# Conv and attention in fp32: 140 unused products of zeros between the attention and the last output projections

## The chip, the core and the metric

The kernel runs on one core of one Trainium2 chip, in one launch. The metric is the device time of a whole execution in microseconds (us). Before the change two runs took 2857.51 and 2857.95 us, median 2857.73 us.

## What is computed

The input `x` has 4 images of 384 channels and 48 x 48 positions, so 4 x 2304 tokens. All of it is fp32.

```python
local = depthwise_conv_7x7(x) * bn_scale + bn_shift
qkv   = layernorm(x_tokens) @ qkv_w.T + qkv_b          # 8 heads of 48
q     = q + layernorm(local_tokens)
out   = softmax(q @ k.T * 48**-0.5) @ v
y     = x + (out @ proj_w.T + proj_b)
```

## The kernel before

**Tiling.** A group `t` is 384 tokens (`G`), six groups to an image, 24 in all (`NT`). For each group the kernel goes over 4 pairs of heads `p` and 18 key blocks `kb` of 128 keys. `score` (L786) makes four products of 64 keys x 384 queries for a pair and a block (L795), and ScalarE takes the exponential of the two banks at once (L803). `weigh` (L808) makes the four products of the values with these exponentials (L816). Each of these products uses a quarter of TensorE's array: 48 or 64 rows by 64 columns. `project` (L501, its matmul is L503) makes the linear layers with the whole 128 x 128 array, three products to one 128 x 384 result, and the last three outputs of a group go through `finish` (L768), where VectorE adds bias and residual (L771) and ScalarE's queue sends the store (L774). `columns` (L618, its matmul is L624), at the start, has products of one row by 128 columns, with the row in three different strips of 32 partitions.

In the trace every fp32 product leaves two MATMUL records and two LDWEIGHTS records, so the x counts there are twice the number of products.

**PSUM.** There are two rings of two buffers, each buffer two banks: `ring()` (named r) and `accumulator()` (named o). `two_banks()` (L96) takes from them in turn.

**Order.** PE, DVE and ACT run in the order in which the code is written (`manual_schedule`, L84 and L85); the queues of SP and POOL are ordered by the scheduler. VectorE's depthwise convolution is dealt out by a plan over points between the attention's steps; none of it is left when the last group `t` = 23 is attended.

**Where the change goes.** After the last attention step stand

```python
    rest()
    pair_out()
    pair_add()
    for before in range(NT - NG, NT):
```

`rest` (L835) issues the last `weigh`, `pair_out` (L690) copies the last pair's first bank (L702, ACT), `pair_add` (L704) adds the second one (L711, DVE) and sends the denominators off (L714 and L718, SP). The loop then makes the output projections of the last image's six groups: 9 products each, with `two_banks()` twice. `divide` (L722) of the last group and its scaling (L1094) are issued inside this loop behind the first and the third group's `finish`; the sixth projection needs them. The tiles with the tags `k0` and `k1` of the pool `big` hold keys of the token groups 0 and 1 of the image in work.

Of the kernel before, what the change touches and what calls it, by code (L numbers as in the profile page):

```python
# [10 lines left out]
F32 = mybir.dt.float32  # L11
# [4 lines left out]
P = 128  # L16
# [29 lines left out]
def unshifted_pass(  # L46
# [16 lines left out]
    nc = tc.nc  # L63
# [3 lines left out]
    CC = C // P  # L67
    G = RG * W
# [10 lines left out]
    big = ctx.enter_context(tc.tile_pool(name="big", bufs=1))  # L79
# [16 lines left out]
    def two_banks():  # L96
        return next(either)()
# [80 lines left out]
    for c in range(CC):  # L178
        for r, n, first in ((0, HD, 0), (64, HD, 1), (48, 16, 6), (112, 16, 7)):
            head = first + 2 * c if first < 6 else first  # L180
            ch = head * HD + (16 * c if first >= 6 else 0)
            while n:
                part = min(n, P - ch % P)
                pieces.append((c, r, ch // P, ch % P, part))
                r, n, ch = r + part, n - part, ch + part
# [315 lines left out]
    def project(dst, weights, src, n=G):  # L501
        for c in range(CC):
            nc.tensor.matmul(dst, lhsT=weights(c), rhs=src(c), start=c == 0, stop=c == CC - 1)  # L503
# [85 lines left out]
    rows = {}  # L589
# [28 lines left out]
    def columns():  # L618

        r, r2 = two_banks(), two_banks()  # L620
        m = {1: r[:, 0, 0:CC], 2: r[:, 1, 0:CC], 0: r2[:, 0, 0:CC]}
        for i in m:
            for c in range(CC):
                nc.tensor.matmul(  # L624
                    m[i][:, c : c + 1],
                    lhsT=row[of_row(i), c * P : (c + 1) * P],
                    rhs=one[of_row(i)],
                    start=True,
                    stop=True,
                )  # L630
        return m, r2[:, 1, :G]
# [58 lines left out]
    def pair_out():  # L690

        if not ended:
            return
        t, p, sums = ended[0]
        if p == 0:
            ao = work.tile([P, CC, G], F32, tag="ao", name=f"ao{t}")
            ao3 = work.tile([P, G], F32, tag="aot", name=f"aot{t}", bufs=1)
            den = dram.tile([NH, G], F32, tag="den", name=f"den{t}")
            outputs[t] = ao, ao3, den
        ao, ao3, den = outputs[t]  # L700
        dst = ao[:, p, :] if p < CC else ao3
        nc.scalar.copy(dst[0 : 64 + HA], sums[0 : 64 + HA, 0, :G])  # L702

    def pair_add():  # L704

        if not ended:
            return
        t, p, sums = ended.pop()
        ao, ao3, den = outputs[t]
        dst = (ao[:, p, :] if p < CC else ao3)[0 : 64 + HA]  # L710
        nc.vector.tensor_add(dst, sums[0 : 64 + HA, 1, :G], dst)  # L711
        for j in range(2):
            r = 64 * j
            nc.sync.dma_start(out=den[2 * p + j : 2 * p + j + 1], in_=dst[r + HD : r + HA])  # L714
        if p == NP - 1:
            for c in range(CC):
                for r in (0, 64):
                    nc.sync.dma_start(  # L718
                        out=ao[r + HD : r + 64, c, :], in_=ao3[r + 16 * c : r + 16 * c + 16]
                    )  # L720

    def divide(t):  # L722

        few = NH * G // P
        rd = work.tile([P, few], F32, tag="rd", name="rd")
        rb = work.tile([P, CC, G], F32, tag="rb", name="rb", bufs=1)
        rden = dram.tile([NH, G], F32, tag="rden", name=f"rden{t}")
        nc.sync.dma_start(out=rd, in_=outputs[t][2].rearrange("h (k f) -> (h k) f", f=few))
        nc.vector.reciprocal(rd, rd)

        for bound, op in ((SAFE, ALU.is_le), (1 / SAFE, ALU.is_ge)):
            nc.vector.scalar_tensor_tensor(inside, rd, bound, inside, op, ALU.mult)
        nc.sync.dma_start(out=rden.rearrange("h (k f) -> (h k) f", f=few), in_=rd)
        heads = rden[0:6].rearrange("(c h) n -> h c n", h=2)
        for j in range(2):
            r = 64 * j
            last = rden[6 + j : 7 + j].rearrange("o (x n) -> o x n", x=1)
            nc.sync.dma_start(
                out=rb[r : r + HD], in_=heads[j : j + 1].to_broadcast([HD, CC, G])
            )  # L740
            nc.sync.dma_start(out=rb[r + HD : r + 64], in_=last.to_broadcast([16, CC, G]))
        return rb
# [25 lines left out]
    def finish(t, co, m, queue=nc.sync):  # L768
        b, g = divmod(t, NG)
        xr = residuals[t]  # L770
        nc.vector.scalar_tensor_tensor(  # L771
            xr[:, co, :], m, pb[:, co : co + 1], xr[:, co, :], ALU.add, ALU.add
        )
        queue.dma_start(  # L774
            out=out[b, co * P : (co + 1) * P, g * G : (g + 1) * G], in_=xr[:, co, :]
        )
# [4 lines left out]
    halves = [slice(64 * i, 64 * i + 64) for i in range(2)]  # L781
# [26 lines left out]
    def weigh():  # L808
        nonlocal sums
        t, p, kb, pt = weighing.popleft()  # L810
        if kb == 0:
            sums = accumulator()
        for i, h in enumerate(halves):
            for j in range(2):
                first = (kb % NB * NH + 2 * p + j) * HA
                nc.tensor.matmul(  # L816
                    sums[halves[j], i, :G],
                    lhsT=values[t // NG, kb // NB][h, first : first + 64],
                    rhs=pt[h, j, :],
                    start=kb == 0,  # L820
                    stop=kb == KB - 1,
                )
        if kb == KB - 1:
            ended.append((t, p, sums))

    def attend(t, s, half):
# [3 lines left out]
        for kb in range(k0 + n * half, k0 + n * half + n):  # L830
            score(t, p, kb)
            if len(weighing) > LAG:
                weigh()

    def rest():  # L835
        while weighing:
            weigh()
        while jobs:
            jobs.popleft()()
# [52 lines left out]
    m, bank = columns()  # L892
# [57 lines left out]
    for t in range(NT):  # L950
        b, g = divmod(t, NG)
        if g == 0 and b:
# [4 lines that stand above are left out]
# [46 lines left out]
        for s in range(NSLOT):  # L1003
# [66 lines left out]
            if following and s == first + 1:  # L1070
                norm.sum_squares()
                if t:
                    norm.out()

    rest()
    pair_out()
    pair_add()
    for before in range(NT - NG, NT):
        ao = aos[before % NG]
        if before == NT - NG + 3:  # L1080
            judge[1](two_banks()[:, 0, :])
        r, r2 = two_banks(), two_banks()
        parts = r[:, 0, :G], r[:, 1, :G], r2[:, 0, :G]
        for co, m in enumerate(parts):
            project(m, lambda c: w_o[:, c, co * P : (co + 1) * P], lambda c: ao[:, c, :])
        for co, m in enumerate(parts):
            finish(before, co, m, nc.scalar)
        if before == NT - NG:
            rb = divide(NT - 1)
            judge[0]()  # L1090
        if before == NT - NG + 3:
            judge[2]()
        if before == NT - NG + 2:
            nc.vector.tensor_mul(outputs[NT - 1][0], outputs[NT - 1][0], rb)  # L1094
        if before == NT - 2:
            n_outside = judge[3]()
# [3 lines left out]
def conv_attention(tc: tile.TileContext, *args):  # L1100
    nc = tc.nc
    few = NH * RG * 48 // P
    with tc.tile_pool(name="keep", bufs=1) as keep:
        inside = keep.tile([P, few], F32, tag="inside", name="inside")
        outside = keep.tile([P, few], F32, tag="outside", name="outside")
        ones = keep.tile([P, 1], F32, tag="ones_col", name="ones_col")
        total = keep.tile([1, 1], F32, tag="total", name="total")
        flag = keep.tile([1, 1], mybir.dt.int32, tag="flag", name="flag")
        counts = []
        nc.vector.memset(inside, 1.0)  # L1110
        nc.vector.memset(ones, 1.0)

        def compare():
            nc.vector.tensor_scalar(outside, inside, 0.5, None, ALU.is_lt)

        def count(m):
            counts.append(m[0:1, :few])
            nc.tensor.matmul(counts[0], lhsT=ones, rhs=outside, start=True, stop=True)

        def decide():  # L1120
            nc.vector.tensor_reduce(total, counts[0], AX.X, ALU.add)
            nc.vector.tensor_copy(flag, total)

        def read():
            return nc.values_load(flag[0:1, 0:1])

        n_outside = unshifted_pass(tc, *args, inside, (compare, count, decide, read))
        with tc.If(n_outside > 0):
            shifted_pass(tc, *args)
# [505 lines left out]
```

## Time and profile before

| what | value |
|---|---|
| median of 2 runs | 2857.73 us |
| span of the profiled execution, first to last instruction | 2857.6 us |
| mean granted TensorE clock | 0.997 |
| PE busy | 2838.7 us, 99% of the span |
| PE weight loads (PEld) busy | 1778.1 us, 62% |
| VectorE busy | 2344.6 us, 82% |
| ScalarE busy | 1649.5 us, 58% |
| last attention product on PE starts | 2816.62 us |
| first record of the last projections | 2817.03 us |
| last VectorE instruction starts | 2852.51 us |

The profiled execution shows no time of its own outside its span, so 2857.6 us is compared with the median of 2857.73 us.

How to read it: a row of a timeline has start, length, engine, source line, operation, result<-operands, rows*columns of the array for TensorE, shapes and the number of instructions merged into it. "L816" is line 816 of the kernel. The length of a MATMUL record is modelled and has a latency in it, so what one product takes in a stream is read from the distance between starts, or from the chain of waits, whose rows have start, length, engine, line and count. PEld is the load of weights, which can run under the matmul before it.

### The profile page before, as it was taken

To read this page: it belongs to the slowest core of one execution; us is meant where nothing else is said; L and a number is where in the kernel's file an instruction comes from. 1 tells how busy PE (TensorE), PEld (TensorE's weight loads), DVE (VectorE), ACT (ScalarE), POOL (GpSimd) and SP (SyncE) were. 2 spreads that over 40 slices of the span, in tenths; PEclk is the share of its full clock that TensorE was granted. 3 is DMA by queue.
4 is the path that set the end of the run, shared out by engine and by line. 5 is a ranking of instruction groups with operands and counts; after the bars stand their busy time and mean duration, and the time that the engine had idled before them with its cause. 6 is when DMAs were issued, how large, how long until landed. Compare 5 with 4: busy or idle time off the path is not lost.

```text
span 2857.6 us, 70328 instructions
## 1 busy us (share of the span) xinstructions
PE 2838.7 (99%) x29558; PEld 1778.1 (62%) x29558; DVE 2344.6 (82%) x4635; ACT 1649.5 (58%) x2350; POOL 14.9 (1%) x77
## 2 busy tenths in 40 slices
PE   9999999999999999999999999999999999999999
PEld 5544444654554466666655546888875545788886
DVE  7899999999888988878888889887788787887401
ACT  4366666666226666666622666666652366666662
POOL 1000000000000000000000000000000000000000
PEclk9999999999999999999999999999999999999999
DMA  5101121112231211121132112101113211111111
GB/s 106 40 5 36 45 49 35 36 26 43 71 83 25 46 35 41 31 39 24 38 94 70 28 30 50 36 22 37 44 25 94 53 20 29 43 23 32 46 38 63
DMA packets 103433, 123.71 MB, mean 43 GB/s; under 512 B 43136, under 2 KB 89152, under 8 KB 103104
## 3 DMA queue, kind: packets, MB, share of 16 engines
q1 hardware_dynamic: 99568, 115.48, 17.0%
q8 instruction: 234, 3.83, 0.6%
q10 hardware_dynamic: 2992, 3.62, 0.4%
q14 instruction: 95, 0.78, 0.1%
q0 software_dynamic: 544, 0.01, 0.0%
HBM read 81.39 MB, written 27.03 MB: 38 GB/s over the span
## 4 chain that ended last, share of the span: by engine, by line
PE 92%; DVE 6%; DMA 0%; POOL 0%; ACT 0%; issue 0%; DVEq 0%; ACTq 0%; POOLq 0%
PE o L816 37%; PE r L795 37%; PE o L503 9%; PE r L503 9%; DVE acc L284 5%; DMA pb<-in_proj_b_dram 0%; PE r L299 0%; PE r L412 0%; ACT pt L803 0%; DVE sq L401 0%; DVE xn L681 0%; DMA parts<-part 0%; DVE sq L400 0%; POOL qk_vec L167 0%; DVE acc L672 0%
## 5 line engine op out<-in xcount | busy, mean ns | idle before, releaser
L803 ACT ACTIVATE pt<-r 128x768 f32<-128x768 f32 x1728 | 1399.6, 810 | 760.1 <-PE r L795 743.6
L284 DVE SCALAR_TENSOR_TENSOR acc<-slab,vec,acc 128x368 f32<-128x368 f32 (+6 forms) x3447 | 1756.3, 582 | 1.2
L816 PE MATMUL o<-pt,v 64*64 64x384 f32 x13824 | 1544.7, 483 | 0.0
L795 PE MATMUL r<-xn,k 48*64 48x384 f32 x10368 | 1157.8, 483 | 3.7 <-ACT pt L803 3.7
L816 PEld LDWEIGHTS o<-pt,v 64*64 64x64 f32 x13824 | 715.3, 133 | 406.7 <-issue 224.0
L795 PEld LDWEIGHTS r<-xn,k 48*64 48x64 f32 x10368 | 531.9, 133 | 316.2 <-issue 176.1
L795 PE MATMUL r<-qt,kt 48*64 48x384 f32 x3456 | 388.1, 482 | 0.1
L795 PEld LDWEIGHTS r<-qt,kt 48*64 48x64 f32 x3456 | 181.3, 133 | 99.1 <-issue 43.8
L711 DVE TENSOR_TENSOR ao<-o,ao 113x384 f32<-113x384 f32 x72 | 39.9, 554 | 194.0 <-PE r L795 176.8
L503 PE MATMUL o<-xn,w_qk 128*128 128x384 f32 x450 | 153.3, 486 | 0.0
L503 PE MATMUL r<-xn,w_qk 128*128 128x384 f32 x414 | 141.1, 486 | 0.0
L503 PEld LDWEIGHTS o<-xn,w_qk 128*128 128x128 f32 x450 | 85.5, 190 | 59.6
L503 PEld LDWEIGHTS r<-xn,w_qk 128*128 128x128 f32 x414 | 78.7, 190 | 54.8
L536 ACT COPY v<-r 128x384 f32<-128x384 f32 x42 | 18.2, 482 | 126.9 <-PE r L503 126.9
L503 PE MATMUL r<-w_v,xn 128*128 128x384 f32 x252 | 85.2, 487 | 0.0
L711 DVE TENSOR_TENSOR aot<-o,aot 113x384 f32<-113x384 f32 x24 | 13.3, 556 | 82.4 <-ACT aot L702 64.8
L503 PE MATMUL o<-af,w_o 128*128 128x384 f32 x222 | 75.0, 487 | 0.0
L400 DVE TENSOR_TENSOR sq<-sq 128x384 f32<-128x384 f32 x47 | 26.0, 554 | 57.7 <-ACT sq L395 56.2
L503 PEld LDWEIGHTS r<-w_v,xn 128*128 128x128 f32 x252 | 47.6, 190 | 34.4 <-issue 1.8
L503 PE MATMUL o<-w_v,xn 128*128 128x384 f32 x180 | 64.4, 498 | 1.3 <-ACT w_v L635 1.3
L503 PEld LDWEIGHTS o<-af,w_o 128*128 128x128 f32 x222 | 42.1, 190 | 29.2
L771 DVE SCALAR_TENSOR_TENSOR xr<-r,pb,xr 128x384 f32<-128x384 f32 x27 | 16.4, 617 | 51.8 <-ACT xn L555 41.9
(139 smaller groups left out, 1036.9 us busy)
## 6 DMA issues: line engine op xcount, KB each, us to landing
xr<-in_x_dram SPq DMA_DIRECT2D x24, 576.0 KB
slab<-in_x_dram SPq DMA_DIRECT2D x32, 378.0 KB
held<-ao SPq DMA_DIRECT2D x20, 576.0 KB
af<-held SPq DMA_DIRECT2D x20, 576.0 KB
rb<-rden SPq DMA_DIRECT2D x48, 216.0 KB
out_dram<-xr SPq DMA_DIRECT2D x54, 192.0 KB
xn<-in_x_dram SPq DMA_DIRECT2D x46, 216.0 KB
slab<-in_x_dram SPq DMA_DIRECT2D x14, 297.0 KB
```

The costliest lines, as they stand in the source:

```text
L284: nc.vector.scalar_tensor_tensor(dst, src, weight, dst, ALU.mult, ALU.add)
L400: nc.vector.tensor_add(self.buf[:, 0, :], src[:, 0, :], src[:, 1, :])
L503: nc.tensor.matmul(dst, lhsT=weights(c), rhs=src(c), start=c == 0, stop=c == CC - 1)
L536: nc.scalar.copy(v[:, blk, :, 0:HD], r[:, :C].rearrange("p (h d) -> p h d", d=HD))
L711: nc.vector.tensor_add(dst, sums[0 : 64 + HA, 1, :G], dst)
L771: nc.vector.scalar_tensor_tensor(xr[:, co, :], m, pb[:, co : co + 1], xr[:, co, :], ALU.add, ALU.add)
L795: nc.tensor.matmul(r[h, j, :G], lhsT=kk[:, blk * P + h.start : blk * P + h.stop], rhs=qq, start=True, stop=True,)
L803: nc.scalar.activation(pt, r[:, :, :G], AF.Exp, scale=SCALE)
L816: nc.tensor.matmul(sums[halves[j], i, :G], lhsT=values[t // NG, kb // NB][h, first : first + 64], rhs=pt[h, j, :], start=kb == 0, stop=kb ...
```

## The change

A new function `halves_first` is called between `pair_add()` and the last loop. It fills two tiles with zeros on POOL, one declared float32r and one fp32, under the tags `k0` and `k1`, and issues products of them into PSUM buffers that nobody reads. In order: 24 float32r products of 64 x 128 row tiles that alternate between the upper and the lower rows (`j`) with new weights for each pair; 24 with two moving tiles per weights, `j` innermost; 24 with `j` outside, so that the same rows come twice in a row; 12 float32r products of the whole array; and four rounds of 6 row-tile products followed by 8 fp32 products of 64 x 64. That is 108 float32r products and 32 fp32 ones. The results of the reference are computed as before.

```diff
+    def halves_first():
+
+        part = big.tile([P, CC, G], mybir.dt.float32r, tag="k0", name="part_r")
+        whole = big.tile([P, CC, G], F32, tag="k1", name="whole_f")
+        nc.gpsimd.memset(part.bitcast(F32), 0.0)
+        nc.gpsimd.memset(whole, 0.0)
+
+        def rows(j):
+            return slice(64 * j, 64 * j + 64)
+
+        def row_tile(r, j, w, m):
+            nc.tensor.matmul(
+                r[:, j, :G],
+                lhsT=part[rows(j), w, 0:P],
+                rhs=part[rows(j), m, :],
+                start=True,
+                stop=True,
+            )
+
+        def quad(r):
+            for j in range(2):
+                for h in halves:
+                    nc.tensor.matmul(
+                        r[h, j, :G],
+                        lhsT=whole[rows(j), 0, h],
+                        rhs=whole[rows(j), 1, :],
+                        start=True,
+                        stop=True,
+                    )
+
+        r = two_banks()
+        for i in range(12):
+            for j in range(2):
+                row_tile(r, j, i % 3, (i + 1) % 3)
+        r = two_banks()
+        for i in range(6):
+            for m in range(2):
+                for j in range(2):
+                    row_tile(r, j, i % 3, m)
+        r = two_banks()
+        for i in range(6):
+            for j in range(2):
+                for m in range(2):
+                    row_tile(r, j, i % 3, m)
+        r = two_banks()
+        for i in range(12):
+            nc.tensor.matmul(
+                r[:, i % 2, :G],
+                lhsT=part[:, i % 3, 0:P],
+                rhs=part[:, (i + 1) % 3, :],
+                start=True,
+                stop=True,
+            )
+        for n in range(4):
+            r = two_banks()
+            for w, m in ((0, 0), (0, 1), (1, 2)):
+                for j in range(2):
+                    row_tile(r, j, w, m)
+            r = two_banks()
+            for _ in range(2):
+                quad(r)
...
     rest()
     pair_out()
     pair_add()
+    halves_first()
     for before in range(NT - NG, NT):
```

## The prediction, made before the changed kernel ran

> **What bounds the kernel now.** I read the busy times first, then the chain of waits around the place of the change, then single rows there. Busy times of the page and its chain by engine:
>
> ```profile
> PE 2838.7 (99%) x29558; PEld 1778.1 (62%) x29558; DVE 2344.6 (82%) x4635; ACT 1649.5 (58%) x2350; POOL 14.9 (1%) x77
> PE 92%; DVE 6%; DMA 0%; POOL 0%; ACT 0%; issue 0%; DVEq 0%; ACTq 0%; POOLq 0%
> ```
>
> TensorE is full and carries the chain. An average says nothing of the last 40 us, where the change goes, so here is the chain there (start, length, what):
>
> ```profile
> 2813.87 0.65 PE o L816 x4
> 2814.52 0.65 PE r L795 x4
> 2815.17 1.94 PE o L816 x18
> 2817.11 4.07 PE r L503 x12
> 2821.17 1.94 PE o L503 x6
> 2823.11 3.87 PE r L503 x12
> ...
> 2850.53 1.95 PE r L503 x6
> 2852.48 0.02 issue
> 2852.51 0.62 DVE xr L771
> ```
>
> PE is the chain up to 2852.48 with no gap in it. So whatever PE does at 2817.1 is added to the end in full. Three prices stand in these rows. Six whole-array fp32 products (12 records) take 3.87 us in a stream: 0.645 each, 0.3225 a record. Four 64 x 64 fp32 products take 0.65 us together (0.648), as long as one whole-array product: the four quarters of the array work side by side. And the first projection row has 4.07 where a later one has 3.87: 0.20 us is the price of going from quarters to the whole array. Its parts are in the timeline (start, length):
>
> ```profile
> 857.40 0.49 PE L503 MATMUL o<-ao,w_o 128*128 128x384 f32 x1
> 857.82 0.53 PE L795 MATMUL r<-xn,k 48*64 48x384 f32 x1
> 2816.62 0.48 PE L816 MATMUL o<-pt,v 64*64 64x384 f32 x2
> 2817.03 0.19 PEld L503 LDWEIGHTS r<-af,w_o 128*128 128x128 f32 x1 [0.60 <-issue]
> 2817.03 0.59 PE L503 MATMUL r<-af,w_o 128*128 128x384 f32 x1
> ```
>
> Last record to first load is 0.41 to 0.42 in both directions, of which 0.32 is streaming: 0.09 of drain. Then the first load is bare, and the first record is that much longer than its kind: 0.59 against 0.49, so about 0.105 with 128 columns, and 0.53 against 0.48, so 0.05 with 64. A switch costs 0.20 into 128 columns and 0.14 into 64.
>
> **What the Trainium skill says.** "TensorEngine Tiling (Array Packing)", Tiling Modes: changing the mode drains the engine, and tiles load and multiply independently. The rows above agree: 0.09 us of drain, four quarters in the time of one. "FP8 and Floating Point Precision", TensorE Precision Notes: fp32 takes four passes; a reduced form reads 4 bytes and truncates. The first agrees, 0.645 / 4 = 0.161 us for a pass of 384; no float32r product is in this trace. "TensorE: Matmul & The Clock Gate", Back-to-back issue gap: 384 / 2.4 + 2.5 ns = 0.1625 us, an estimate from that page beside 0.161 measured. Same page, LDWEIGHTS: columns / 1.2, so 0.107 us for 128, beside the 0.105 above.
>
> **The change part by part.** Nothing is removed. In the built program the products stand in the written order between L816 and the first L503; DVE and ACT keep their order, SP keeps its own, and POOL gets two memsets behind all its others.
>
> *POOL.* A 128 x 128 memset took 0.205 us, so nine times that is about 1.9 us each. They wait for the last readers of the keys in `k0` and `k1`: pair 2, blocks 2 and 5 of the last group. Block 17 of that pair is scored at about 2791, a block each 1.30 us, so these are at about 2772 and 2776. Both memsets are done by about 2778, nearly 40 us ahead of their reader. Cost nothing; late, they would show as a wait of PE for POOL.
>
> *Buffers.* The first `r` and `o` are free as they are today. The fourth call (the whole-array part) takes the accumulator of the last pair and waits for L711, done at 2818.2; it starts after 6 us of row tiles. Later calls wait for PE's own writes four calls back, done long before. Twelve calls keep the turn of r and o as it was. Cost nothing.
>
> *A pass in float32r.* I take one pass, 0.161 us; the bounds are one and four (0.645). *Row tiles.* Two of 64 x 128 take the rows and columns that four quarters take in the attention, and write two banks side by side as those do, so I take 0.161 a pair. That asks for a 128-column load per tile and pass. Two places speak to it: packing, 14 records of 50 moving columns on the whole array (a row of the groups), and `columns`, 18 records of one moving column in three strips (four rows of the timeline).
>
> ```profile
> L207 PE MATMUL o<-natural,packing 128*128 128x50 f32 x14 | 1.7, 270 | 0.0
> ```
>
> ```profile
> 32.20 0.74 PE L624 MATMUL o<-one,row 1*128 1x1 f32 x8
> 32.70 0.27 PE L624 MATMUL r<-one,row 1*128 1x1 f32 x1
> 32.78 0.27 PE L624 MATMUL o<-one,row 1*128 1x1 f32 x2
> 33.06 0.47 PE L624 MATMUL r<-one,row 1*128 1x1 f32 x3
> ```
>
> Packing is bound by its loads: (1.7 - 0.27) / 13 = 0.11 us a load, under the 0.161 of a pass, so it hides in one array. In `columns` all 18 start between 32.20 and about 33.28, 1.1 us where one after another would need 2.0: 128-column loads of different row strips overlap, and the third strip (r) starts before the second (o) is through its list. So a strip whose list is held up doesn't stop the next, which is what the third order needs. As to issue, a pair of row tiles asks for two load-and-multiply records in 0.161 us; the attention has eight in 0.648, the same rate.
>
> *The sum.* Three orders: 3 x 12 pairs x 0.161 = 5.81. Whole array: 12 x 0.161 = 1.94. Four rounds: 4 x 3 pairs x 0.161 = 1.94 and 8 sets of four fp32 quarters x 0.645 = 5.16. Switches: six into 128 columns (first order, whole array, four rounds) x 0.197 = 1.18, four into 64 columns x 0.144 = 0.58; the last one into the projections is paid today. Together 16.6 us.
>
> *Behind it.* All six projections, their `finish` and their stores move by the same 16.6 us, and with them `divide`, which stands behind the first group's L771 on DVE. Its reply is needed at 2846, after a scaling that ends at 2836.6: almost 10 us of slack that keep their size. The last store (5 us from L771 to the end of the span) moves along. So 2857.6 + 16.6 = 2874.2 for the profiled execution; the median of the runs shown is 0.1 above the span: 2874.3.
>
> **The rivals.**
> *Row tiles take turns*, for a bank, a queue or float32r's own reasons, in some or all orders. For it: no trace shows a float32r tile, and the third order sends two of a tile in a row. Against it: `columns` and the quarters. All: 48 passes more, +7.7, 2882.1 us; one order alone: +1.9, 2876.3.
> *Loads come bare*, if float32r's load can't go under a pass: 60 slots (48 pairs, 12 whole) x 0.11 = +6.6, 2880.9. Against it: the loads of L503 start with the matmul before.
> *Four passes*: 60 x 3 x 0.161 = +29.0, 2903.3. Against it: the change is named single-pass, as the page has it of the reduced form.
> *Cheaper switches*: 64 x 64 and 64 x 128 split the rows alike; if going between them doesn't drain, eight switches fall (4 x 0.197 + 4 x 0.144 = 1.4): 2872.9. Nothing here shows this pair.
> *The other side, slower by over 2%*: every row-tile product drains before the next starts, because it changes tile. Price: drain 0.09, bare load 0.105, pass 0.161, and the latency of a record beyond its streaming, 0.486 - 0.3225 = 0.164: 0.52 us. 96 x 0.52 = 49.9, with 1.94, 5.16 and 0.8 of switches 57.8: 2915.5. It decides from 0.51 us a product. Against it: quarters change tile at every product and don't.
> *It does nothing or something else* (products not run, something in the tail gained): 2857.7. They stand in the built program; PE has no slack to hide them.
>
> **How the numbers follow.** About what a measurement can tell from no change is 2%, 57 us. Chances: the forecast 0.62 (its own range, from 15 to 19 us added: 2872.7 to 2876.7), cheaper switches 0.08, turns 0.14, bare loads 0.08, four passes 0.04, a drain each 0.02, nothing or else 0.02. The range from 2872.3 to 2882.6 holds the first four, 0.92, and ends there because turns in all orders sit at its upper end. Over 2% slower: the drain, and four passes together with turns (2934), 0.02. Faster by 2%: 0.01. Within: 0.97.
>
> **What would show it.** In the profile after: L846 (row tiles) with starts of both tiles within 0.02 us and 1.94 us for each of the three orders, the same for all three; L881 1.94 us; L857 0.645 for four; 0.09 us between the last streaming and the next load at each change of mode; no wait of PE for POOL; the first L503 at about 2833.6 instead of 2817.03 and the rows behind it as far apart as now. An order at 3.9 us means turns, at 3.2 bare loads, at 7.7 four passes. The prediction is wrong if PE's rows there are not the chain, or if the projections behind come out longer.

## The result, and the profile after

Two runs of the changed kernel took 2878.47 and 2880.12 us, median 2879.3, against 2857.73 before: ratio 1.0074, 95% interval 1.0045 to 1.0104. In five later runs (e2 below), beside 17 of the kernel before, it took 2875.9 against 2858.88: 1.0060, interval 1.0047 to 1.0074. The forecast was 2874.3 us, with a range from 2872.3 to 2882.6 that left room for rivals, and from 2872.7 to 2876.7 for the forecast alone.

The profiled execution has a span of 2876.6 us; that same run took 2878.47. Between 1.7 and 1.9 us lie outside the span in every run for which both are known, so a span is compared with a span from here on, and a run with a run. For the kernel before, the profiled execution and the two timed runs were different executions: a span of 2857.6 us beside a median of 2857.73 doesn't mean that nothing lies outside the span.

The page after, busy times and the chain by engine:

```profile
PE 2858.0 (99%) x29730; PEld 1834.7 (64%) x29730; DVE 2344.1 (81%) x4635; ACT 1650.0 (57%) x2350; POOL 17.0 (1%) x79
PE 93%; DVE 6%; ACT 0%; DMA 0%; issue 0%; SPq 0%; DVEq 0%; ACTq 0%
```

PE has 172 records more: 108 for the float32r products, one each, and 64 for the 32 fp32 ones, two each. So a float32r product isn't split into two records as an fp32 one is. The chain of waits at the place of the change (start, length, what):

```profile
2816.61 1.94 PE o L816 x17
2818.54 2.28 PE r L846 x24
2820.83 2.08 PE o L846 x24
2822.91 2.08 PE r L846 x24
2824.99 2.29 PE o L881 x12
2827.28 0.72 PE r L846 x6
2828.00 1.45 PE o L857 x16
...
2833.80 0.72 PE r L846 x6
2834.52 1.45 PE o L857 x16
2835.97 4.07 PE r L503 x12
2840.03 1.94 PE o L503 x6
2841.97 3.87 PE r L503 x12
```

What the reader is to see: the inserted rows fill 2818.54 to 2835.97, 17.43 us, with no gap; the three orders take the same 2.08 (the first one has the switch of 0.20 on top); and from L503 on every row has the length it had before, the 4.07 of the first one too. The last L771 starts at 2871.37 and the span ends 5.2 us later, as before (5.1). POOL's two memsets are the rows

```profile
2774.03 1.06 POOL L839 MEMSET part_r<- 128x1152 f32 x1 [654.70 <-PE r L795]
2777.92 1.06 POOL L840 MEMSET whole_f<- 128x1152 f32 x1 [2.83 <-PE r L795]
```

done at 2779, nearly 40 us ahead of their reader.

### The profile page after: what moved, and what is told of

Its sections match the earlier page's. It is cut to its first block, busy times and chain, and to the rows that moved or that the text cites. A ratio compares the mean times of both kernels' runs of the same rounds, so it can differ in the third digit from the quotient of the medians.

```text
span 2876.6 us, 70682 instructions
## 1 busy us (share of the span) xinstructions
PE 2858.0 (99%) x29730; PEld 1834.7 (64%) x29730; DVE 2344.1 (81%) x4635; ACT 1650.0 (57%) x2350; POOL 17.0 (1%) x79
## 4 chain that ended last, share of the span: by engine, by line
PE 93%; DVE 6%; ACT 0%; DMA 0%; issue 0%; SPq 0%; DVEq 0%; ACTq 0%
PE r L795 37%; PE o L816 37%; PE o L503 9%; PE r L503 9%; DVE acc L284 5%; PE r L846 0%; PE r L299 0%; PE o L857 0%; DMA staged<-in_qkv_wT_dram 0%; ACT pt L803 0%; PE r L412 0%; SPq L104 0%; DVE sq L401 0%; DMA slab<-in_x_dram 0%; DVE sq L400 0%
## 5 line engine op out<-in xcount | busy, mean ns | idle before, releaser
L816 PE MATMUL o<-pt,v 64*64 64x384 f32 x13824 | 1565.5, 483 | 0.0
L795 PE MATMUL r<-xn,k 48*64 48x384 f32 x10368 | 1171.6, 483 | 3.9 <-ACT pt L803 3.9
L816 PEld LDWEIGHTS o<-pt,v 64*64 64x64 f32 x13824 | 740.4, 133 | 384.7 <-issue 198.6
L795 PEld LDWEIGHTS r<-xn,k 48*64 48x64 f32 x10368 | 549.4, 133 | 299.2 <-issue 159.2
L795 PE MATMUL r<-qt,kt 48*64 48x384 f32 x3456 | 394.5, 482 | 0.1
L795 PEld LDWEIGHTS r<-qt,kt 48*64 48x64 f32 x3456 | 188.0, 133 | 93.9 <-issue 33.2
L503 PE MATMUL o<-xn,w_qk 128*128 128x384 f32 x450 | 154.3, 488 | 0.0
L503 PE MATMUL r<-xn,w_qk 128*128 128x384 f32 x414 | 141.0, 486 | 0.0
L503 PEld LDWEIGHTS o<-xn,w_qk 128*128 128x128 f32 x450 | 86.1, 191 | 60.5 <-issue 1.5
L503 PEld LDWEIGHTS r<-xn,w_qk 128*128 128x128 f32 x414 | 78.7, 190 | 54.9
L503 PE MATMUL r<-w_v,xn 128*128 128x384 f32 x252 | 85.2, 487 | 0.0
L711 DVE TENSOR_TENSOR aot<-o,aot 113x384 f32<-113x384 f32 x24 | 13.4, 556 | 82.4 <-ACT aot L702 64.8
L771 DVE SCALAR_TENSOR_TENSOR xr<-r,pb,xr 128x384 f32<-128x384 f32 x27 | 16.4, 617 | 73.2 <-ACT xn L555 44.8
L503 PE MATMUL o<-af,w_o 128*128 128x384 f32 x222 | 75.0, 486 | 0.0
L503 PEld LDWEIGHTS r<-w_v,xn 128*128 128x128 f32 x252 | 47.6, 190 | 34.4 <-issue 1.8
L503 PE MATMUL o<-w_v,xn 128*128 128x384 f32 x180 | 66.6, 512 | 1.8 <-ACT w_v L635 1.8
L503 PEld LDWEIGHTS o<-af,w_o 128*128 128x128 f32 x222 | 42.1, 190 | 29.2
```

The costliest lines, as they stand in the source:

```text
L771: nc.vector.scalar_tensor_tensor(xr[:, co, :], m, pb[:, co : co + 1], xr[:, co, :], ALU.add, ALU.add)
L795: nc.tensor.matmul(r[h, j, :G], lhsT=kk[:, blk * P + h.start : blk * P + h.stop], rhs=qq, start=True, stop=True,)
L816: nc.tensor.matmul(sums[halves[j], i, :G], lhsT=values[t // NG, kb // NB][h, first : first + 64], rhs=pt[h, j, :], start=kb == 0, stop=kb ...
```

## The experiments

All of them keep the computation of the outputs whole; e2 is the changed kernel itself, the others change only what `halves_first` issues. The edits are shown without the definitions of their small functions, and the comments in them are added here. e3 to e8 are one execution each, so what is read from them is rows of the chain and starts in the timeline, not medians.

### How much of the difference is the change

```diff
@@ e1_memsets_only: halves_first @@
         nc.gpsimd.memset(part.bitcast(F32), 0.0)
         nc.gpsimd.memset(whole, 0.0)
-        r = two_banks()
-        for i in range(12):
...
```

> The new function keeps its two memsets of zeros and makes none of the 140 products. Theory (the 17.4 us that the inserted rows take in the chain are all of the change; the other 1.4 us of the profiled span and the rest of the timed 21.6 us are differences between executions at the start): same as before, ratio within 1.0010, and the changed kernel 17 to 19 us above it. Rival (the two memsets or the longer program cost something of their own): 2 to 4 us above before, and the changed kernel only 17.4 us above this one.

> The changed kernel once more, unaltered, in more rounds. Theory (17.4 us plus chance at the start): 17 to 19 us above before, ratio 1.0060 to 1.0067. Rival (something beside the products): 21 to 22 us again, ratio 1.0075.

The memsets alone: 2858.24 us in 13 runs, ratio 0.9999, interval 0.9991 to 1.0008. The changed kernel again: 17.0 us over before, and 17.7 over the memsets alone. So the rival falls, though not by much in e2 alone (its interval ends at 1.0074, the rival wanted 1.0075), and the first pair of medians (21.6 us apart) had 4 us of something else in it. The chain in the profile of e2 shows the same inserted rows, 2816.52 to 2833.96, 17.44 us:

```profile
2814.59 1.94 PE o L816 x17
2816.52 2.30 PE r L846 x24
...
2833.96 4.07 PE r L503 x12
```

but everything starts 2.0 us earlier than in the first profile. It goes back mainly to the granted clock of TensorE at the start (busy times in a window; the third number from the end is the clock). The first 145 us before, after, and in e2:

```profile
0.00:145.00 145.00, 138.92 (x508) 85.28 (x512) 122.52 (x248) 61.90 (x136) 11.89 (x41) 0.99 0.36 73
```

```profile
0.00:145.00 145.00, 139.61 (x494) 85.53 (x495) 119.64 (x243) 60.31 (x133) 11.89 (x41) 0.96 0.38 72
```

```profile
0.00:145.00 145.00, 137.64 (x516) 84.21 (x516) 123.23 (x249) 62.32 (x137) 11.90 (x41) 1.00 0.40 73
```

0.96 against 1.00 over 145 us is about 5 us of clock withheld. Here is one stretch of it in the first profile after, and the row of the chain that it falls into:

```profile
16.41:19.81 3.40, 3.40 (x7) 1.75 (x6) 3.30 (x9) 3.34 (x14) 0.00 (x0) 0.50 1.10 168
```

```profile
16.04 5.18 PE o L503 x10
```

Ten records of 0.3225 us would be 3.2 us; they took 5.18. The first product of the values (L816) started at 149.7 us in this execution and at 146.3 in e2, so the two were 3.4 us apart there. The Trainium skill, "TensorE: Matmul & The Clock Gate", Part 1, has a clock gate with free-running windows that puts an idle array to half clock. The trace agrees: the clock was 0.50 for 3.4 us, and in the 3.4 us before that PE had been busy for 1.6.

The ten profiled executions of this study, with nearly the same code ahead of the change, show what this does to the end. All their stretches of 3.4 us at half clock lie in the first 330 us, apart from those behind the last projection. With five of them (the first profile after) the last attention row of the chain started at 2816.6; with four (before and e7) at 2815.2 and 2815.0; with three (e4 and e6) at 2813.9 and 2814.3; with two (e1, e3, e5 and e8) between 2812.3 and 2812.9. e2 has two as well and started at 2814.6; some 1.3 us of that are another loss, between 400 and 660 us, where its PE was busy for 258.7 of 260 us and that of the others without a gap. It makes the 3.4 us between the first two profiles of the changed kernel 2.0. So the start of the last attention row moves by over 4 us for reasons ahead of the change, and the same changed kernel had both five stretches and two. Why an execution gets more or fewer of them isn't shown.

### What a float32r pass costs

```diff
@@ e3_sizes: halves_first, in place of the 140 products @@
+        for n in (512, 448, 384, 320, 256, 128):
+            one_pass(n)       # 24 float32r products, whole array, n moving columns
+        for n in (512, 384, 256, 128):
+            four_passes(n)    # 24 fp32 ones
```

> In place of the 140 products: 24 whole-array float32r products for each of the moving sizes 512, 448, 384, 320, 256 and 128, then 24 fp32 ones for each of 512, 384, 256 and 128; weights new for every product. It asks what the 0.0125 us are by which a float32r pass of 384 (0.1735) is longer than a pass of fp32 (0.161). Theory A (a fixed price for each change of weights): 0.226 at 512, 0.200 at 448, 0.147 at 320, 0.120 at 256. Theory B (float32r streams at a lower rate, in proportion): 0.231 at 512, 0.202 at 448, 0.145 at 320, 0.116 at 256. Theory C (the next load is usable only 0.171 after it starts, so the load is the bound): 0.216 at 512, 0.189 at 448, 0.173 at 320 and at 256 and at 128. All: fp32 at 4 x N / 2.4 plus 5 ns, so 0.858, 0.645, 0.432; at 128 A and B have 0.112 for float32r, bound by the loads.

```profile
2814.41 5.69 PE r L872 x24
2820.09 4.86 PE o L872 x24
2824.96 4.19 PE r L872 x24
2829.14 3.51 PE o L872 x24
2832.66 2.88 PE r L872 x24
2835.53 2.63 PE o L872 x24
2838.17 20.65 PE r L884 x48
2858.82 15.48 PE o L884 x48
```

Each row of the chain is one size. Divided by 24 (the first less 0.20 for the switch): 0.229, 0.203, 0.175, 0.146, 0.120, 0.110. fp32 has 0.860 and 0.645 for 512 and 384, the same 0.645 for these zeros as for the data of L503; the difference of 0.215 us for 4 x 128 columns is 0.42 ns a column and pass, the 1 / 2.4 ns of the forecasts. Less N / 2.4 the float32r rows leave 0.015, 0.016, 0.015, 0.013, 0.013 for the sizes down to 256. At 128 it is 0.110, close to the 0.112 of a record of fp32 (5.36 / 48) and to the 0.11 that the prediction read from packing with 50 columns, as it would be if the loads are the bound there.

Theory C falls: it wanted 0.173 at 256. The row means alone don't part A from B, since 0.229 at 512 lies between their 0.226 and 0.231. But they include an irregular beginning of each row. The timeline's starts in the second half of each row are 0.2267, 0.2030, 0.1733, 0.1467 and 0.1200 apart: 0.013 over N / 2.4 at 512, 384, 320 and 256, and 0.016 at 448. The excess doesn't shrink when the size is halved, so it is a fixed price, theory A's form, with 448 the one size that has a little more. Whether it belongs to any single pass was the next question.

```diff
@@ e4_kinds: halves_first, in place of the 140 products @@
+        for kind in (bf16_128, r_128, r_64, bf16_rows, r_upper, r_lower_only):
+            r = two_banks()
+            for i in range(24):
+                kind(r, i)    # 384 moving columns each
```

> In place of the 140 products: 24 products each, all with 384 moving columns, of bf16 on the whole array, float32r on the whole array, float32r with 64 columns of weights, bf16 in 64 x 128 row tiles in turn, float32r in the upper row tile alone, float32r in the lower alone. If the excess over 0.161 belongs to any single pass with new weights (theory A): bf16 0.1735 too, float32r with 64 columns 0.1735. If it belongs to float32r's data (theory B): bf16 0.162, float32r 0.1735 with 64 columns as well. If it is the weight load (theory C): float32r with 64 columns 0.162, bf16 0.162 to 0.1735. One row tile alone: 0.1735 a product, so 4.2 us for 24, if the two tiles of a pair ran side by side in the changed kernel (24 products in 2.08); 2.1 us if a lone tile ran at twice the speed and the pair had taken turns. bf16 row tiles in turn: half of bf16's whole-array time a product.

```profile
2815.81 4.01 PE r L869 x24
2819.82 4.19 PE o L878 x24
2824.01 4.16 PE r L887 x24
2828.17 2.06 PE o L908 x24
2830.22 3.64 PE r L846 x21
```

bf16 (L869) has 0.159 a product if a switch of 0.20 is taken off its row, and 4.01 / 24 = 0.167 if none is, against float32r's 0.175 (L878). The timeline settles it: from bf16's first record (2815.75) to its last (2819.49) 23 steps are 0.163 each, and once steady 0.1625. That is 384 / 2.4 ns and 2.5 ns more; a record of fp32 has 2.5 ns over its two passes as well (0.3225). With 64 columns of weights (L887) float32r has 0.173: half the load changes nothing. So the price isn't every single pass's, nor does it go with the number of columns loaded; of this experiment's three theories B is left, float32r's data.

The row tiles answer the largest doubt of the prediction. The upper tile alone (L846) has 21 products in 3.64 us, 0.173 each, so 24 would be 4.2; in the changed kernel 24 products over both tiles took 2.08. The two tiles of a pair run fully side by side. bf16 row tiles in turn (L908): 2.06 for 24, which is 12 x 0.1625 and 0.11 for the switch. In the whole array the switch into bf16 was 0.11 too (4.01 - 24 x 0.1625), against 0.20 into fp32 or float32r with as many columns. And between the two lone parts the timeline shows this:

```profile
2833.53 0.44 PE L899 MATMUL o<-part_r 64*128 64x384 f32 x1
2833.70 0.33 PE L846 MATMUL r<-part_r 64*128 64x384 f32 x1
2833.82 0.33 PE L899 MATMUL o<-part_r 64*128 64x384 f32 x1
2833.87 0.33 PE L846 MATMUL r<-part_r 64*128 64x384 f32 x1
```

L899, the lower tile, stands in the program behind all 24 of L846. It starts while three products of the upper tile are still to start (2833.70, 2833.87 and 2834.05). So a free tile took work from behind three products in the list. The third order (two of the same rows in succession) needs a reach of one product, and in the changed kernel its starts come in pairs, the first two of them within 0.02 us of 2822.74. That fits its cost, the same as the first order's.

```diff
@@ e6_alternate: halves_first, in place of the 140 products @@
+        for i in range(24):
+            (r_128, bf16_128)[i % 2](r, i)
+        r = two_banks()
+        for i in range(24):
+            (r_128, f_128)[i % 2](r, i)
```

> In place of the 140 products: 24 whole-array products of 384 columns that are float32r and bf16 in turn, then 24 that are float32r and fp32 in turn. It asks where the 0.011 us sit by which a float32r product of any size is longer than a bf16 one. Theory S (in its stream): 0.1735 from a float32r start to the next start, 0.1625 from a bf16 start to the next. Theory L (in the load of its weights, which runs under the product before): 0.1625 from a float32r start, 0.1735 from a bf16 start. Both: a pair 0.336, and with fp32 0.1735 + 0.645 = 0.8185. Rival (a change of type on the array costs by itself): a pair of more than 0.36 with bf16 and more than 0.85 with fp32.

In the chain the 23 rows from 2816.59 to 2820.65 take 4.06 us, a pair 0.353: above the 0.336 of both theories and just under the 0.36 at which I would have called it a price for changing type. Its rows are, for example,

```profile
2816.59 0.18 PE r L869
2816.77 0.17 PE r L878
```

0.17 to 0.18 for both kinds. The pair is 0.017 above the sum of one product of each, so neither S nor L is borne out. How the pair splits isn't certain, since the chain's rows go by the modelled ends; whether it is bf16 that becomes slower beside float32r is not shown. With fp32 a pair takes (2830.49 - 2820.65) / 12 = 0.820, as forecast (0.8185). This experiment was inconclusive on where the price sits.

```diff
@@ e8_strips: halves_first, in place of the 140 products @@
+        for i in range(12):
+            for k in range(4):
+                strip((r, r2)[k // 2], k % 2, k, i)   # rows 32k to 32k + 31
+        r = two_banks()
+        for i in range(24):
+            one_column(r, i)                          # lhsT=part[:, i % 3, 0:1]
```

> In place of the 140 products: 48 float32r products of 32 x 128 in four row strips in turn, each strip into a bank of its own, then 24 float32r products of the whole rows with one column of weights. First part, theory (strips side by side at 0.1735 each, issue no bound): 12 x 0.1735 = 2.08 us and 0.20 for the switch. Rival (TensorE takes a load and a multiply no faster than the 0.081 us that the attention's quarters need): 48 x 0.081 = 3.9. Second part: 0.1735 a product again if the 0.011 us over bf16 belong to every float32r product whatever its weights; 0.1625 if they belong to loading many columns of weights.

Four strips side by side: from 2814.20 to 2816.51 in the chain, 2.31 us with the switch, so 2.11 for 48 products, 0.176 for four. TensorE takes a load and a multiply every 0.044 us here, and issue is no bound at the 0.081 that the row tiles of the change need. One column of weights:

```profile
2816.51 4.29 PE r L876 x24
2820.80 3.87 PE r L503 x12
```

(4.29 - 0.09 for the drain of the switch) / 24 = 0.175. So the price stays with one column of weights, with 64 and with 128, on 32, 64 and 128 rows. It goes with the float32r product. Every product here loaded its weights anew, so whether the price falls due at the load, whatever its size, or in the stream is not parted.

### What a switch is

```diff
@@ e5_switches: halves_first, in place of the 140 products @@
+        for n in range(4):
+            pairs_r(two_banks())   # 3 pairs of float32r row tiles
+            pairs_f(two_banks())   # 2 pairs of fp32 row tiles, same 64 x 128
+        for n in range(4):
+            quad(two_banks())      # 4 fp32 quarters, 64 x 64
+            pairs_f(two_banks())
```

> In place of the 140 products: four rounds of 3 float32r row-tile pairs and 2 fp32 row-tile pairs (both 64 x 128: the type changes, the shape of the tiles doesn't), then four rounds of 4 fp32 quarters of 64 x 64 and 2 fp32 row-tile pairs (the shape changes, the type doesn't). Theory (the shape of the tiles makes a switch, the type doesn't): first half without drain, a round 3 x 0.1735 + 2 x 0.645 = 1.81 us and at most 0.05 more; second half with 0.145 into the quarters and 0.20 into the row tiles, a round 0.645 + 1.29 + 0.345 = 2.28 us. Rival 1 (the type makes the switch): first half 1.81 + 0.40 = 2.21, second half 1.935. Rival 2 (both): 2.21 and 2.28.

```profile
2816.49 0.52 PE r L846 x6
2817.01 1.29 PE o L866 x8
...
2824.22 0.81 PE r L857 x8
2825.03 1.49 PE o L866 x8
```

A round of the first half is 0.52 + 1.29 = 1.81, with nothing for the change of type; one of the second half 0.81 + 1.49 = 2.30. The same L866 row costs 1.29 behind row tiles and 1.49 behind quarters. So going between quarters and row tiles makes a switch, and the type alone doesn't: two tile shapes of 64 rows are different shapes all the same, and the prediction's "cheaper switches" rival falls.

The number of weight columns on full rows is less clear. Going from 128 to 64 of them in float32r cost nothing (L887 in e4), nor did going from one to 128: in e8 the first row of L503 behind L876 has 3.87. But in the kernel before, two records of fp32 with one column do pay:

```profile
2834.72 0.14 PE r L1118 x2
2834.86 4.07 PE o L503 x12
```

Here L503 has the 0.20 of a switch on top. No run varies the type alone with one column of weights, so the cause of this difference stays open.

```diff
@@ e7_grouped: the four rounds of the changed kernel @@
         for n in range(4):
             r = two_banks()
             for w, m in ((0, 0), (0, 1), (1, 2)):
                 for j in range(2):
                     row_tile(r, j, w, m)
+        for n in range(4):
             r = two_banks()
             for _ in range(2):
                 quad(r)
```

> The changed kernel with all 140 products, but the 24 row-tile products of the four rounds ahead of all the 32 quarters: six switches of the array fewer. Theory (a switch costs 0.205 into row tiles and 0.16 into quarters in the chain of the changed kernel): the inserted rows take 17.43 - 3 x 0.205 - 3 x 0.16 = 16.3 us from the end of the attention to the first projection. Rival (what looks like a switch is the start of a new PSUM buffer, and with it a wait for PE's own earlier writes): 17.4, since the buffers change as often.

```profile
2816.94 2.28 PE r L846 x24
...
2825.68 0.72 PE r L846 x6
2826.40 0.52 PE o L846 x6
...
2827.96 1.45 PE r L857 x16
2829.41 1.29 PE o L857 x16
...
2833.28 4.07 PE r L503 x12
```

From 2816.94 to 2833.28: 16.34 us, as forecast. Only the first row of a mode pays, 0.20 and 0.16; a new PSUM buffer with its wait on PE's own older writes costs nothing. It is the cheaper of the two orders tried, and still 16.3 us more than the kernel before.

## Why the prediction was right, step by step

*PE carries the end, and everything behind moves along.* Right: the inserted 17.43 us stand in the chain without a gap, and the rows of L503 behind them kept their lengths. The first L503 record started at 2835.90, not at 2833.6: 0.8 us are the sum's error, 1.4 the later end of the attention (2815.17 to 2816.61 in the chain).

*Work hidden at no cost.* POOL's memsets and the buffers' waits showed nothing in PE's waits, and e1 measured 0.9999. The memset took 1.06 us where I had put 1.9, which didn't matter.

*Row tiles side by side in all three orders.* Right, and for the reason given from `columns`: 2.08 for each order, against 4.2 that a lone tile would need. The rival of turns falls by e4; that of bare loads falls, as it wanted 3.2 us for an order, and half the columns of weights change nothing; four passes and a drain at each product fall by the 2.08.

*Switches.* 1.76 us were put for ten. Measured 0.20 into 128 columns as forecast, and 0.16 into the quarters in place of 0.144: 0.1 us in all.

*A pass in float32r.* This term of the sum was mis-sized: "I take one pass, 0.161 us". It is 0.1735 (2.08 / 12). Over 60 slots that is 0.75 us. 16.6 + 0.75 + 0.1 = 17.45, and 17.43 was measured. The formula that the prediction took from the Trainium skill (0.1625) is short for float32r in the same way; it holds for bf16 in e4.

*From the span to the median.* "The median of the runs shown is 0.1 above the span: 2874.3" treated the profiled execution as one with 0.1 us around it. The runs for which both are known have 1.7 to 1.9 around it; by that, the profiled execution of before was itself some 1.7 us slower than the two timed ones. The result of 2879.3 is 5.0 above the forecast. Of that, 0.8 is the sum's error and 1.8 the time outside the span. The remaining 2.4 are in the spans: 2876.6 and 2878.2 have a mean of 2877.4, where 2857.6 + 17.4 would be 2875.0. In the profiled one of the two, 1.4 us is the later end of the attention; the other has no profile.

So the first result lies above the 2876.7 at which the forecast's own range ended, for reasons ahead of the change that the prediction didn't consider. It lies inside the stated range because that left room for rivals which didn't come true, and that is luck. What was right for its reasons is the price of the inserted products, 16.6 forecast and 17.43 measured, and with it the time added in the larger sample, 17.0 us (interval 13.4 to 21.2).

What stays open: why a float32r product costs 0.011 us more than bf16 or a record of fp32. e3, e4 and e8 show that it is nearly the same for every moving size down to 256 and every shape of weights tried; e6 couldn't place it in the stream or the load.

## What to carry to other kernels

When TensorE is the chain, price inserted work as slots x pass + switches, and count a switch between whole array, row tiles and quarters, not where only the type changes in one of the first two; group products by shape. Row tiles of float32r cost half a whole-array product each (two of 64 rows) or a quarter (four of 32 rows) here, where each strip had a bank of its own; two products in succession for the same rows cost nothing. Before a difference under 1% is explained, measure how far two executions of the same kernel lie apart, and read the price from rows of the chain: the inserted rows took 17.43 and 17.44 us in two executions, where the medians of the changed kernel lie 3.4 us apart.

## What the runs showed of the hardware that was not expected

For N moving columns from 256 to 512 a float32r product took N / 2.4 ns and 13 to 16 ns more (0.1733 us for 384), where bf16 had 2.5 ns more (0.1625 for 384). bf16's record of a weight load is 98 ns for 128 columns where float32r's is 188 and fp32's 190 (mean of the loads in e4), and the switch into bf16 is 0.11 us where the others have 0.20. Going from 128 to 64 columns of weights on full rows (L878 to L887 in e4) costs no switch: the 4.16 us of L887 hold 24 products at 0.173.
